# Two layers of attention over an image: key batches taken ahead, the mean taken early, and another order at the end

## The chip, the cores and the metric

The kernel runs on one core of a Trainium2 chip. The metric is the device time of one execution in microseconds (us); the time given for a kernel is the median of its runs. The engines are TensorE (PE, with its weight loads as PEld), VectorE (DVE), ScalarE (ACT), GpSimd (POOL) and SyncE (SP, which issues the DMAs here). Each engine takes its instructions in the order in which the program lists them for it.

## The reference

Two layers run one after the other on x of shape (4, 128, 96, 96), float32. A layer is, with all biases left out here:

```python
g     = maxpool2(conv1x1(x, g_w))        # (b, 64, 2304)
theta = conv1x1(x, theta_w)              # (b, 64, 9216)
phi   = maxpool2(conv1x1(x, phi_w))      # (b, 64, 2304)
attn  = softmax(theta^T phi)             # (b, 9216 queries, 2304 keys)
y     = attn g^T                         # (b, 9216, 64)
x     = batchnorm(conv1x1(y, W_w)) + x
```

So there are eight attention blocks (four images, two layers), each of 9216 queries, 2304 keys and 64 channels.

## The kernel before

The eight blocks run in an order (`ORDER`) that alternates images, so that the keys of a block can be made while the block in front of it runs. A block's queries are cut into nine pairs of 2 x 512 queries (`Pair`), its keys into 18 tiles of 128 (`KT`). A step `t` of the main loop takes one batch of two key tiles (`KB`) for one pair; nine steps (`NB`) make a pair, and 18 steps (`CYCLE`) make a cycle of an even and an odd pair. `s` is the step's place in its cycle. The order of everything is written out by hand in this loop, and each engine keeps it.

In a step, PE computes two tiles of scores (L313) and, for the batch of one step earlier, two tiles of values (L336). All these matmuls have 64x64 tiles, four of which use the four quadrants of the array at once. ACT takes exp of each score tile (L319) from one of two PSUM tiles into one of seven buffers (`EXPS`), with a fixed shift, not with the row's maximum. DVE adds the exps up over the key tiles (L326, L328). Beside that, a cycle holds for the two pairs before it: the two halves of the sum, over the partitions, are brought together by a DMA on SP (`move`, L365) and an addition (`fold`, L369); ones turn them into denominators (L446), ACT copies these out (L360), DVE takes reciprocals in pieces of 128 columns (L356), multiplies (L380), PE projects with W (L386), and DVE adds the shift and x (L395). `note` (L373) sums the reciprocals on ACT for a check at the end: if a sum of exps left the range of float32, a general kernel runs instead.

The keys of a block: PE multiplies a chunk of x by the weights of g and phi into a PSUM tile of a ring of two (`ps_misc`), DVE pools it to 128 keys (L225). From the pooled phi the mean over some keys is taken off, which leaves the softmax as it is: `centring` (L266, L267) takes the mean on DVE, `centred` (L272) subtracts it on ACT, `copied` (L278) puts phi on the other 64 partitions too. `square` (L285) transposes g on DVE in pieces of 32x32 into gT, which the values need. For blocks after the first, `chunks` makes a batch of two key tiles crosswise in 64x64 tiles, half of the contraction in one step, half in the next; the steps are those of `KEYS`. After three batches (`spreads`), phi is centred and copied and g transposed for six tiles at once, and the first time the mean is taken then, over six tiles.

For the first block, two batches of keys are made before the loop by `pooled` (in 128x64 tiles, L238), with theta (L300) between them. In the loop, step t then makes batch t + 2, in the same way, and every third step transposes six tiles of g. In the last cycle, theta of the odd pair (L300) and the denominators of the even pair (L349) have 128x64 tiles; the even pair's reciprocals are taken in a row in step 10 and its projection stands in step 16. After the last scores come the denominators of the last pair, its last two value tiles, and `finish`: copy, add, multiply, project, add x, store in four pieces.

Of the kernel before, what the change touches and what calls it, by code (L numbers as in the profile page):

```python
# [35 lines left out]
NB = NKT // KB  # L36
KEYS = (15, 17, 31)
# [10 lines left out]
def shifted_blocks(ctx: ExitStack, tc: tile.TileContext, x: bass.AP, layers, out: bass.AP, flag):  # L48
# [43 lines left out]
    dens = const.tile([P, len(ORDER) * NP], F32, name="dens")  # L92
    recs = const.tile([P, len(ORDER) * NP], F32, name="recs")
# [109 lines left out]
    class Block:  # L203
# [28 lines left out]
        def pooled(self, j):  # L232

            pss = two_banks(f"gphi_ps_{self.name}_{j}")
            for i in range(2):
                rhs = self.chunk(j * KB + i, slice(0, P))
                for c in range(2):
                    nc.tensor.matmul(  # L238
                        pss[i][ts(c, CI), :], lhsT=self.w.gphi[:, ts(c, CI)], rhs=rhs,
                        start=True, stop=True,  # L240
                    )
            for i in range(2):
                self.pool(j * KB + i, pss[i])
# [35 lines left out]

        def square(self, i, k):  # L280

            tiles = ts(i, GT)
            g = self.gphi[:CI, :].rearrange("p (t k) -> p t k", k=KT)
            for c in range(CI // 32):
                nc.vector.transpose(  # L285
                    self.gT[ts(k, 32), tiles, ts(c, 32)], g[ts(c, 32), tiles, ts(k, 32)]
                )

    class Pair:
# [8 lines left out]
        def theta(self, ps):  # L298
            for h in range(2):
# [3 lines left out]
                )  # L303

# [40 lines left out]
        def denominators(self, ps):  # L345
            parts = [self.sum, self.es[NKT - 1]] if self.last else [self.sum]
            for i, part in enumerate(parts):
                for h in range(2):
                    nc.tensor.matmul(  # L349
                        ps[ts(h, CI), :], lhsT=ones, rhs=part[:, ts(h, QT)],  # L350
                        start=(i == 0), stop=(i == len(parts) - 1),
                    )

# [48 lines left out]
        def finish(self, den, check, result):  # L402

            n = QT // 2
            halves = work.tile([P, PT], F32, tag="halves", name=f"halves_{self.name}")
            y, half = halves[:, :QT], halves[:, QT:]
            nc.scalar.copy(half, self.av[:, QT:])
            nc.vector.tensor_add(y, self.av[:, :QT], half)
            for i in range(2):
                nc.vector.tensor_mul(y[:, ts(i, n)], y[:, ts(i, n)], self.rc[:, ts(i, n)])  # L410
            nc.scalar.activation(
                self.th, den, AF.Identity, accum_out=dens[:, self.number : self.number + 1]
            )
            self.note(self.th)
            pss = [
                ps_sc.tile([P, PT], F32, tag="sc", name=f"W_ps_{self.name}_{i}") for i in range(2)
            ]
            for i in range(2):
                for c in range(2):
                    for h in range(2):  # L420
                        nc.tensor.matmul(
                            pss[i][ts(c, CI), h * QT : h * QT + n],
                            lhsT=self.blk.w.W[ts(h, CI), ts(c, CI)],
                            rhs=y[ts(h, CI), ts(i, n)], start=True, stop=True,
                        )
            check()
            for i in range(2):
                for h in range(2):
# [3 lines left out]
                        dst, pss[i][:, h * QT : h * QT + n], self.blk.w.shift, dst,  # L432
                        op0=ALU.add, op1=ALU.add,
                    )
                    nc.sync.dma_start(out=self.blk.store[:, first : first + n], in_=dst)
                if i == 0:
                    result()

    def denominators(both, folded):
# [3 lines left out]
        def make():  # L443
            for h in range(2):
                for i in range(2):
# [5 lines left out]
        def take():  # L451
            for i in range(2):
                both[i].take_denominators(pss[i], both[i].halves[:, QT:])
# [61 lines left out]
    busy(WARM[1])  # L515
    ws[0].make_theta()
    b0.pooled(0)
    first_cols(ps_sc.tile([P, PT], F32, tag="sc", name="cols_first_ps")[:, :QT])
    th = ps_sc.tile([P, PT], F32, tag="sc", name="theta_ps_0")[:, :QT]
    pairs[0].theta(th)  # L520
    b0.centring(KB)
    b0.centred(ts(0, KB * KT))
    b0.copied(ts(0, KB * KT))
    pairs[0].take_theta(th)
    for w in ws:
        w.make_std()
    nc.scalar.preload_act_table(AF.Exp)
    b0.pooled(1)
    b0.centred(ts(1, KB * KT))
    b0.copied(ts(1, KB * KT))  # L530
# [8 lines left out]
    keys, spreads = {}, {}  # L539
    for n in range(1, len(blocks)):  # L540
        cycle = (n - 1) * NP * NB // CYCLE * CYCLE
        for j in range(NB):
            t = cycle + KEYS[j % len(KEYS)] + j // len(KEYS) * CYCLE
            keys[t] = (n, j)
            if j % len(KEYS) == len(KEYS) - 1:
                spreads[t + 2] = (blocks[n], j // len(KEYS))
    loads = {4 * NB + 4: 2, 31 * NB + 4: 3}
    late = len(pairs) - 2
    folded, gone, pending = None, [], (None, None)
    for t in range(total + 1):  # L550
# [4 lines left out]
        if t in keys:  # L555
            n, i = keys[t]
            if i == 0:
                begin(n)
            first, *pending = blocks[n].chunks(i)
        elif t < total and s == (THETAS if q else THETAS + 2):  # L560
            if q < late:
                first, *pending = thetas(pairs[q + 1 : q + 3])
            else:
                ps = ps_misc.tile([P, QT], F32, tag="misc", name="theta_ps_last")
                first, take = (lambda: odd.theta(ps)), (lambda: odd.take_theta(ps))
        elif gone and s == SUMS:
            second, take = denominators(gone, folded)
        elif gone and s in PROJECT:
            pair = gone[PROJECT.index(s)]
            second, take = pair.multiply, pair.add  # L570
        if t < total:
# [4 lines left out]
            if s == NB and q < late:  # L576
# [13 lines left out]
        if t + 2 < NB:  # L590
            b0.pooled(t + 2)
# [5 lines left out]
        if t + 2 < NB:  # L597
            b0.centred(ts(t + 2, KB * KT))
            b0.copied(ts(t + 2, KB * KT))
            if t % 3 == 0:  # L600
                for k in range(KT // 32):
# [372 lines left out]
```

## Time and profile before

| | |
|---|---|
| median of 3 runs | 2544.60 us (2544.17 to 2545.17) |
| the profiled execution's own time | 2544.58 us |
| its span, first to last instruction | 2542.5 us |
| PE busy | 2525.2 us, 99% |
| DVE busy | 2170.6 us, 85% |
| ACT busy | 1625.2 us, 64% |
| one exp of a score tile (L319) | 1112 ns, 1296 of them |
| one addition of exps (L328) | 1224 ns |
| pooling of a key tile (L225) | 684 ns |
| reciprocal of 128 columns (L356) | 946 ns (3.38 us for four in a row) |

A row of the trace gives start, length, engine, line, operation and tiles; a bracket at its end tells how long the engine was idle before it and which work ended that. A row with xN holds N instructions in a row. A 64x64 matmul of 512 columns appears as two records, so that 16 records are two tiles of scores. Rows of stages give, for each engine, busy time and number of instructions, then the granted clock of PE (1.00 is full speed) and the DMA's share.

### The profile page before, as it was taken

Reading aid. Unit: us, or ns where it says so; the run is one execution under the profiler, and the core shown is the slowest. Engines: PE = TensorE matmul, PEld = TensorE weight load, DVE = VectorE, ACT = ScalarE, POOL = GpSimd, SP = SyncE. Lnnn points to the kernel's source line nnn. Section 1 sums busy time; section 2 is a strip of 40 time slices with the busy share of each in tenths; the row PEclk is TensorE's granted clock in tenths of the full one; section 3 lists DMA queues with packets and bytes.
Section 4 is the critical chain, followed back from the end, with each engine's and each line's share of the span. In section 5 each row is a group of like instructions: output and inputs, shape, how many; then the busy total and the mean of one; then the engine's idle time right before and its main releaser. Section 6 shows DMA issues by size and latency. Waiting matters only on the chain.

```text
span 2542.5 us, 53323 instructions
## 1 busy us (share of the span) xinstructions
PE 2525.2 (99%) x23290; PEld 1380.7 (54%) x23290; DVE 2170.6 (85%) x2258; ACT 1625.2 (64%) x1792; POOL 0.7 (0%) x6
## 2 busy tenths in 40 slices
PE   9999999999999999999999999999999999999998
PEld 3345555455555555555555555555555545555552
DVE  6788888888888888888888888888888888888888
ACT  5666666666666666666666666666666666666665
POOL 0000000000000000000000000000000000000000
PEclk9999999999999999999999999999999999999999
DMA  4020000000000000020000000000000000000000
GB/s 157 6 84 10 10 9 6 9 10 10 10 10 21 26 26 26 14 84 10 10 10 18 13 26 26 26 18 5 10 10 10 18 26 14 26 26 26 26 26 35
DMA packets 16581, 59.86 MB, mean 24 GB/s; under 512 B 2634, under 2 KB 3540, under 8 KB 16340
## 3 DMA queue, kind: packets, MB, share of 16 engines
q1 hardware_dynamic: 16172, 56.31, 7.2%
q8 instruction: 184, 3.01, 0.5%
q14 instruction: 57, 0.47, 0.1%
q10 hardware_dynamic: 168, 0.07, 0.0%
HBM read 19.14 MB, written 18.87 MB: 15 GB/s over the span
## 4 chain that ended last, share of the span: by engine, by line
PE 97%; DVE 2%; ACT 1%; issue 0%; POOL 0%; DVEq 0%; POOLq 0%
PE sc L313 43%; PE av L336 43%; PE gphi_ps L199 4%; PE W_ps L386 2%; PE theta_ps L199 2%; PE den_ps L446 1%; DVE sum L328 1%; ACT exp L319 1%; PE gphi_ps L238 0%; ACT phi L272 0%; DVE centre L266 0%; DVE gT L285 0%; DVE gphi L225 0%; PE warm_ps L508 0%; DVE sum L356 0%
## 5 line engine op out<-in xcount | busy, mean ns | idle before, releaser
L319 ACT ACTIVATE exp<-sc,nshift 128x1024 f32<-128x1024 f32 x1296 | 1384.3, 1112 | 815.3 <-PE sc L313 814.8
L328 DVE TENSOR_TENSOR sum<-sum,exp 128x1024 f32<-128x1024 f32 x1151 | 1408.3, 1224 | 261.9 <-ACT exp L319 208.9
L313 PE MATMUL sc<-theta,phi 64*64 64x512 f32 x10368 | 1470.0, 589 | 0.3 <-ACT theta L307 0.3
L336 PE MATMUL av<-exp,gT 64*64 64x512 f32 x10368 | 1424.7, 589 | 1.0 <-DVE gT L285 1.0
L313 PEld LDWEIGHTS sc<-theta,phi 64*64 64x64 f32 x10368 | 641.3, 133 | 496.4 <-issue 476.2
L336 PEld LDWEIGHTS av<-exp,gT 64*64 64x64 f32 x10368 | 628.9, 133 | 506.9 <-issue 470.2
L356 DVE RECIPROCAL halves<-halves 128x128 f32<-128x128 f32 x280 | 264.9, 946 | 0.0
L199 PE MATMUL gphi_ps<-x,gphiT 64*64 64x512 f32 x1008 | 171.3, 591 | 5.1 <-DVE gphi L225 5.1
L326 DVE TENSOR_TENSOR sum<-exp,exp 128x1024 f32<-128x1024 f32 x72 | 88.1, 1224 | 50.0 <-ACT exp L319 49.6
L225 DVE TENSOR_REDUCE gphi<-gphi_ps 128x128 f32<-128x512 f32 x144 | 93.2, 684 | 39.4 <-PE gphi_ps L199 28.8
L343 ACT COPY halves<-av 128x1024 f32<-128x1024 f32 x71 | 71.9, 1013 | 50.2 <-PE av L336 50.2
L395 DVE SCALAR_TENSOR_TENSOR x<-W_ps,shift,x 128x512 f32<-128x512 f32 x142 | 99.6, 743 | 0.0
L199 PE MATMUL theta_ps<-x,thetaT 64*64 64x512 f32 x560 | 94.4, 589 | 0.0
L199 PEld LDWEIGHTS gphi_ps<-x,gphiT 64*64 64x64 f32 x1008 | 62.2, 132 | 59.1 <-issue 34.1
L386 PE MATMUL W_ps<-halves,WT 64*64 64x512 f32 x568 | 94.2, 589 | 0.0
L369 DVE TENSOR_TENSOR folded<-folded,sum 64x1024 f32<-64x1024 f32 x70 | 85.2, 1216 | 1.1
L285 DVE STREAM_TRANSPOSE gT<-gphi 32x192 f32<-32x192 f32 x192 | 70.7, 368 | 3.6
L386 PEld LDWEIGHTS W_ps<-halves,WT 64*64 64x64 f32 x568 | 36.2, 133 | 27.0 <-issue 27.0
L380 DVE TENSOR_TENSOR halves<-halves 128x512 f32<-128x512 f32 x70 | 48.5, 692 | 2.4
L199 PEld LDWEIGHTS theta_ps<-x,thetaT 64*64 64x64 f32 x560 | 35.6, 133 | 27.2 <-issue 26.9
L446 PE MATMUL den_ps<-folded,ones 64*64 64x512 f32 x280 | 47.1, 589 | 0.0
L377 DVE TENSOR_TENSOR halves<-halves 128x512 f32<-128x512 f32 x71 | 45.7, 684 | 0.0
(89 smaller groups left out, 299.0 us busy)
## 6 DMA issues: line engine op xcount, KB each, us to landing
folded<-sum SPq DMA_DIRECT2D x70, 256.0 KB
out_dram<-x SPq DMA_DIRECT2D x35, 512.0 KB
x<-in_x_dram SPq DMA_DIRECT2D x18, 768.0 KB
x<-in_x_dram SPq DMA_DIRECT2D x12, 384.0 KB
out_dram<-x SPq DMA_DIRECT2D x4, 128.0 KB
gphi_nat<-in_L_conv_phi_w_dram SPq DMA_DIRECT2D x2, 32.0 KB
rows_other<-in_L_conv_g_b_dram SPq DMA_DIRECT2D x4, 0.2 KB
W_nat<-in_L_conv_W_w_dram SPq DMA_DIRECT2D x2, 32.0 KB
```

What stands on the lines that cost most here:

```text
L199: nc.tensor.matmul(out, lhsT=lhsT, rhs=rhs, start=step == 0, stop=step == 1)
L225: nc.vector.tensor_reduce(self.gphi[:, ts(k, KT)].rearrange("p (h w) -> p h w", w=w), ps.rearrange("p (h a w b) -> p h w a b", a=2, b=2, w=w),
L313: nc.tensor.matmul(ps[ts(c, CI), ts(h, QT)], lhsT=self.blk.phi[ts(h, CI), ts(2 * k + c, CI)], rhs=self.th[ts(h, CI), :], start=True, stop= ...
L319: nc.scalar.activation(e, ps, AF.Exp, bias=nshift)
L326: nc.vector.tensor_add(self.sum, self.es[0], e)
L328: nc.vector.tensor_add(self.sum, self.sum, e)
L336: nc.tensor.matmul(self.av[ts(h, CI), ts(r, QT)], lhsT=self.blk.gT[ts(r, CI), k, :], rhs=e[ts(r, CI), ts(h, QT)], start=(k == 0), stop=(k ...
L356: nc.vector.reciprocal(self.rc[:, ts(i, P)], src[:, ts(i, P)])
L369: nc.vector.tensor_add(folded[here, :], folded[here, :], self.sum[here, :])
L386: nc.tensor.matmul(self.pss[h][ts(c, CI), :], lhsT=self.blk.w.W[ts(h, CI), ts(c, CI)], rhs=self.y[ts(h, CI), :], start=True, stop=True,)
L395: nc.vector.scalar_tensor_tensor(dst, self.pss[h], self.blk.w.shift, dst, op0=ALU.add, op1=ALU.add)
L446: nc.tensor.matmul(pss[i][ts(h, CI), :], lhsT=ones[ts(i, CI), :], rhs=folded[ts(i, CI), ts(h, QT)], start=True, stop=True,)
```

## The change

- Before the first scores, six batches of the first block's keys are made (`FIRST = 6`), chunk by chunk with one PSUM tile each; theta of the first pair comes behind them, and the first six tiles of g are transposed there.
- The other three batches are made in the loop, crosswise, by `chunks`, at steps 0, 2 and 4. Their transposes are spread over steps 0 to 6.
- For later blocks, the mean of phi is taken over the first batch alone, two steps behind that batch, and no longer at the first spread.
- In the last cycle, theta of the odd pair and the denominators of the even pair go in 64x64 tiles: the even pair's sum is moved and folded as those of other pairs, and theta's two halves of the contraction lie in two PSUM tiles that DVE adds. The even pair's reciprocals stand in steps 13 to 16, its product in step 16, its projection in step 17.
- In the last three steps, fewer values are computed beside the scores (one tile, one, two); four value tiles remain behind the last denominators, which are made in two halves of 256 columns.
- At the end, both halves of the values are multiplied by the reciprocals straight from PSUM, and the projection adds them up in PSUM. The final check has fewer instructions.

```diff
+FIRST = 6
...
+        def pooled(self, k):
+            ps = ps_misc.tile([P, QT], F32, tag="misc", name=f"gphi_ps_{self.name}_{k}")
+            for c in range(2):
+                nc.tensor.matmul(
+                    ps[ts(c, CI), :], lhsT=self.w.gphi[:, ts(c, CI)],
+                    rhs=self.chunk(k, slice(0, P)), start=True, stop=True,
+                )
+            self.pool(k, ps)
...
+        def batch(self, j):
+            self.centred(ts(j, KB * KT))
+            self.copied(ts(j, KB * KT))
...
+        def theta_alone(self):
+            pss = two_banks(f"theta_ps_{self.name}")
+            def make():
+                for c in range(2):
+                    for r in range(2):
+                        nc.tensor.matmul(
+                            pss[r][ts(c, CI), :], lhsT=self.blk.w.theta[ts(r, CI), :],
+                            rhs=self.blk.xt[ts(r, CI), ts(2 * self.p + c, QT)],
+                            start=True, stop=True,
+                        )
+            def take():
+                self.take_theta(pss[0])
+                nc.vector.tensor_add(self.th, self.th, pss[1])
+            return make, take
...
+        def last_denominators(self):
+            n = QT // 2
+            self.rc, notes = self.sum[:, :QT], []
+            for i in range(2):
+                den = ps_sc.tile([P, PT], F32, tag="sc", name=f"den_last_ps_{i}")[:, :n]
+                for part in (self.sum, self.es[NKT - 1]):
+                    for h in range(2):
+                        nc.tensor.matmul(
+                            den[ts(h, CI), :], lhsT=ones,
+                            rhs=part[:, h * QT + i * n : h * QT + (i + 1) * n],
+                            start=part is self.sum, stop=part is not self.sum,
+                        )
+                notes.append(den)
+            for i in (0, 1):
+                for k in range(n // P):
+                    nc.vector.reciprocal(
+                        self.rc[:, ts(i * n // P + k, P)], notes[i][:, ts(k, P)]
                     )
...
         def finish(self, ...):
-            nc.scalar.copy(half, self.av[:, QT:])
-            nc.vector.tensor_add(y, self.av[:, :QT], half)
             for i in range(2):
-                nc.vector.tensor_mul(y[:, ts(i, n)], y[:, ts(i, n)], self.rc[:, ts(i, n)])
...
+                for r in range(2):
+                    part = slice(r * QT + i * n, r * QT + (i + 1) * n)
+                    nc.vector.tensor_mul(y[:, part], self.av[:, part], self.rc[:, ts(i, n)])
...
+                    for r in range(2):
+                        for h in range(2):
+                            nc.tensor.matmul(
+                                pss[i][h][ts(c, CI), :n],
+                                lhsT=self.blk.w.W[ts(h, CI), ts(c, CI)],
+                                rhs=y[ts(h, CI), r * QT + i * n : r * QT + (i + 1) * n],
+                                start=r == 0, stop=r == 1,
+                            )
...
+    b0.pooled(0)
     ws[0].make_theta()
-    b0.pooled(0)
     first_cols(...)
+    b0.pooled(1)
+    b0.centring(KB)
+    b0.batch(0)
+    for j in range(1, FIRST):
+        for k in range(j * KB, (j + 1) * KB):
+            b0.pooled(k)
+        b0.batch(j)
...
     pairs[0].theta(th)
...
     pairs[0].take_theta(th)
+    for k in range(KT // 32):
+        b0.square(0, k)
...
-    keys, spreads = {}, {}
+    keys = {2 * j: (0, FIRST + j) for j in range(NB - FIRST)}
+    squares = {k: [(1, k)] for k in range(4)} | {k: [(2, 2 * k - 10), (2, 2 * k - 9)] for k in (5, 6)}
+    spreads, centres = {}, {}
...
+            if j == 0:
+                centres[t + 2] = blocks[n]
...
+    ends = {
+        total - 3: (NKT - 8,), total - 2: (NKT - 7,), total - 1: (NKT - 6, NKT - 5),
+        total: range(NKT - 4, NKT),
+    }
...
+        elif q == late and s == 11:
+            second, take = denominators([even], folded)
+        elif t == total - 1:
+            second, take = even.multiply, even.add
...
-            if s == NB and q < late:
+            if s == NB:
                 folded = work.tile([P, PT], F32, tag="folded", name=f"folded_{q}", bufs=1)
                 even.move(folded)
...
+        if q == late and s == 10:
+            even.fold(folded)
...
+        if t - 1 in keys and t < NB:
+            b0.batch(keys[t - 1][1])
...
-            for k in range(j * KB, (j + 1) * KB):
+            for k in ends.get(t, range(j * KB, (j + 1) * KB)):
                 pairs[before].values(k)
...
             if q == late:
                 if s == 10:
-                    den = ps_misc.tile([P, QT], F32, tag="misc", name="den_ps")
-                    even.denominators(den)
-                    even.take_denominators(den, even.sum[:, :QT])
-                    even.inverses(even.rc)
                     even.add_halves()
-                if s == 13:
-                    even.note(even.rc)
+                if s - 13 in range(QT // P):
+                    even.inverses(even.rc, (s - 13,))
+                if s == 16:
                     even.normalise()
-                if s == 16:
-                    even.multiply()
-                    even.add()
...
+        if t in centres:
+            centres[t].centring(KB)
+        for i, k in squares.get(t, []):
+            b0.square(i, k)
...
                 if k == 0:
-                    if i == 0:
-                        blk.centring(GT)
                     blk.centred(ts(i, GT * KT))
```

`second` is issued on PE behind both score tiles of its step and in front of the values; `take` stands on DVE or ACT between the two additions of exps.

## Prediction

> **What bounds the kernel now.** I read the page's busy shares and the shares of its chain, then busy time by stage, then the order of time in the three places where TensorE (PE) is not full: the opening, one spot in each later block, and the end.
>
> ```profile
> PE 2525.2 (99%) x23290; PEld 1380.7 (54%) x23290; DVE 2170.6 (85%) x2258; ACT 1625.2 (64%) x1792; POOL 0.7 (0%) x6
> PE 97%; DVE 2%; ACT 1%; issue 0%; POOL 0%; DVEq 0%; POOLq 0%
> 60.00:342.00 282.00, 281.26 (x2608) 135.40 (x2605) 240.18 (x264) 180.53 (x198) 0.00 (x0) 1.00 0.08 26
> 1752.00:2034.00 282.00, 282.00 (x2633) 165.15 (x2628) 242.29 (x244) 182.98 (x203) 0.00 (x0) 1.00 0.05 11
> ```
>
> PE bounds it; a row of 16 score records (two key tiles) takes 1.72 us, so one unit, four concurrent 64x64 matmuls of 512 columns, is 0.858 us. The change removes no unit in the middle, so it can only win idle or badly filled PE time. The stage rows say that there is little: 0.74 us of idle in the first 282 us window, none in the other shown. The idle sits here:
>
> ```profile
> 160.10 0.95 DVE L266 TENSOR_REDUCE centre<-gphi 64x1 f32<-64x768 f32 x1
> 161.27 0.93 ACT L272 ACTIVATE phi<-gphi,centre 64x768 f32<-64x768 f32 x1 [2.44 <-DVE centre L267]
> 163.48 1.04 PE L313 MATMUL sc<-theta,phi 64*64 64x512 f32 x8
> 164.51 1.28 DVE L225 TENSOR_REDUCE gphi<-gphi_ps 128x128 f32<-128x512 f32 x2
> 165.25 1.25 PE L199 MATMUL gphi_ps<-x,gphiT 64*64 64x512 f32 x5 [0.74 <-DVE gphi L225]
> ...
> 173.46 2.05 PE L313 MATMUL sc<-theta,phi 64*64 64x512 f32 x14
> ...
> 231.65 0.93 ACT L272 ACTIVATE phi<-gphi,centre 64x768 f32<-64x768 f32 x1
> ```
>
> Once per block DVE reduces the mean, ScalarE (ACT) waits 2.44 us for it with the exps behind it, the adds come late, the pooling behind them too, and PE waits for the two PSUM tiles that pooling frees. The last row is the same block's second spread, with the same transposes and pooling but no mean: ACT does not wait, and PE shows no gap after it. The opening and the end:
>
> ```profile
> 7.46 0.69 DVE L225 TENSOR_REDUCE gphi<-gphi_ps 128x128 f32<-128x512 f32 x1 [1.54 <-PE gphi_ps L238]
> 11.45 1.95 PE L313 MATMUL sc<-theta,phi 64*64 64x512 f32 x16 [0.31 <-ACT theta L307]
> 17.33 3.06 DVE L285 STREAM_TRANSPOSE gT<-gphi 32x192 f32<-32x192 f32 x8
> 20.44 1.51 PE L336 MATMUL av<-exp,gT 64*64 64x512 f32 x11 [0.28 <-DVE gT L285]
> 67.89 0.23 PE L110 MATMUL cols_other_ps<-ident,rows_other 11*128 11x11 f32 x1
> ...
> 2503.77 3.38 DVE L356 RECIPROCAL sum<-sum 128x128 f32<-128x128 f32 x4
> 2529.87 3.39 DVE L356 RECIPROCAL sum<-den_last_ps 128x128 f32<-128x128 f32 x4 [2.12 <-PE den_last_ps L349]
> 2534.41 1.09 PE L421 MATMUL W_ps<-halves,WT 64*64 64x256 f32 x16 [2.70 <-DVE halves L410]
> 2536.37 0.85 DVE L431 SCALAR_TENSOR_TENSOR x<-W_ps,shift,x 128x256 f32<-128x256 f32 x2
> ```
>
> **The change part by part.** All sums are against the profiled execution: span 2542.5 us, 2544.58 us with what lies around it, which is the median of the runs (2544.60).
>
> *Opening.* The mark is cols_other (67.89): up to it the same PE work stands in both kernels, and eight units (6.86) and a change of tile shape (0.15) lie between the second pair's first score and the mark, so that score starts at 60.9. From the first keys (5.58) to 60.9 there are 55 units: 18 key chunks, 3 thetas, 18 scores, 16 values, 47.2 us. Before loses 8.1 there.
> After: x lands piece by piece (the first at 5.0, the eighth, which chunk 11 needs, at 14.1, by the trace's landings), in an unchanged order on SP. Chunk 0 starts at 5.2 in front of thetaT, still at the half clock that the records show until about 7 us, and its pooling runs 7.0 to 7.75. Two PSUM tiles rotate, so chunk k+2 waits for the pooling of chunk k: from start to pooled is 1.07 + 0.69, the wait 0.06, hence 0.92 per chunk, slower than PE (0.86) and than x. With the mean (0.42 + 0.15) between poolings 1 and 2, chunk 11 is pooled at 18.9. Then ACT takes the batch (0.50 + 0.40 with issue, 0.94) and only behind it theta (0.69): first score at 20.65, against 11.45. Thirteen units are then done, 42 are left, 36.0 us. Stalls in them: the fourth score waits for an exp, 0.5; the transposes of tiles 12 to 17 stand behind two adds each (2.5) in steps 5 and 6 and end about 52.3, when PE wants them at 51.2, 1.1. The mark's score is at 20.65 + 36.0 + 1.6 = 58.3: **-2.6**. The keys left for the loop run crosswise, in the shape of the scores, so the two changes of shape per step that before pays there are in the 8.1. Bounds: no stall -4.2; the loop at the old pace of 5.47 a step (1.87 keys, 1.88 values, 1.72 scores), no gain.
>
> *Mean early.* It costs DVE 0.57 in a step of 4.29 us that holds 2.5 us of adds and nothing for PE to wait on soon (the next key batch is four steps later); in exchange 1.1 leaves the crowded step. ACT's phi then starts at 158.85 behind its exp, exps run at 160.25, DVE pools at 162.6 and ends at 163.9; PE asks at 164.3. Worth: by idle 0.74 each. By units: from 163.48 to 173.46 lie ten (8.58 us) and 9.98 pass, so 1.4, since one quadrant of PE starts early and three late. The records of the seven blocks agree with the second (from the stall at 165.25 to that at 446.67 are 281.42 us for 326 units, 279.7). I take 1.4: 7 x 1.4 = **-9.8**; bounds -5.2, and 0 if the wait only moves.
>
> *Last cycle.* theta and the even pair's denominators lose their 128x64 shape: two changes each, 2479.12 to 2480.13 for one unit, 0.15 + 0.15, so -0.66 with the other. The sum's halves now go through one more SP transfer (256 KB, 2.8 us to landing elsewhere in the trace; the store in front of it is issued 1.2 us earlier) and a fold of 1.22 on DVE; it lands at 2498.6, DVE arrives at 2498.9: hidden, if late by 1 us, 1 us on DVE. Theta's second half is another 0.69 on DVE, hidden by two steps.
> The cost: reciprocals stand one per step in steps 13 to 16, normalise behind them, and the even pair's projection, which needs it, stands in step 17 right behind the last scores. From the fold on DVE has fold 1.2, 14 adds of 1.27, five reciprocals of 0.83, three short products and sums 1.8, two additions of x 1.3: 26.3, from 2498.9 to 2525.5 with 0.3 of waiting. PE, with two values fewer, ends its last scores at 2522.75. The projection waits: **+2.8**, the values and denominators behind it, and nothing else can run on PE. Bounds +2.4 (DVE never waiting) to +3.3.
> Then the denominators, four value tiles (3.43 us) over the last reciprocals (done 1.2 us before them), and the tail: four products out of PSUM at 0.4 (nearest row 0.38 from SBUF; 0.43 for an addition out of PSUM), projection 1.3 for the first half, four checks 0.65 and additions 0.43: 4.2 us from the last value to the last addition, against 5.5 (2531.71 to 2537.22). -1.3. Copy (0.59) and addition (0.63) of the halves go, as the projection adds them up. The sums for the check, four on ACT of some 0.6 each, end 2533.3, before the last value. The even pair's store comes 2 us later on SP, with 9 us to spare; POOL's queue is as it was. Sum: -0.7 + 2.8 - 1.3 = **+0.9** with rounding.
>
> Total -2.6 - 9.8 + 0.9 = -11.5: span 2531.0, **2533.1 us**.
>
> **A rule that speaks against it.** The 2.70 us gap before the final projection left the clock at full: the 16 records of 256 columns behind it took 1.09 us, as half of 16 score records (0.86) and the last one's end; at half clock it would be over 1.7. The Trainium skill, page "TensorE: Matmul & The Clock Gate", section "Why this matters for your kernels", advises no idle of more than about 3 us between bursts, or the clock falls to half. My new gap is 2.8, with 8 us of PE work behind it. By the row it costs nothing more; by the rule, were the gap counted, one window of about 3.4 us (the same page, "What's actually happening") at half speed, an estimate of +1.7 us, 2534.8. I go by the row, as the gaps are alike; the range keeps the rule.
>
> **The rivals.**
> 1. Only visible idle comes back in the middle (5.2): 2537.7. For it: the stage rows. Against it: the count of units.
> 2. DVE is ready in the last cycle and the projection doesn't wait: 2530.3. For it: DVE shows waits for exps until 2499. Against it: it was behind until 2524.89 in the kernel shown, with its reciprocals in one lump.
> 3. The opening stays at DVE's pace and gains nothing: 2535.7. For it: values waited for gT at 20.44. Against it: 2.5 adds, half of 1.3 pooling, 0.75 transposes, 4 us in a step of 4.29.
> 4. The mean is not what makes pooling late; the stall stays: 2542.9. Against it: the second spread.
> 5. Slower: the 1.8 us without PE work before the first score, at 18.9 to 20.65, comes close behind twelve chunks with small gaps, and the clock falls and stays. At half clock PE loses half of the time, so over 23 us of it turn the sign; 50 us would give 2533.1 + 25 = 2558. Against it: the clock is 1.00 in each stage row, and the longer gap of 2.70 did not lower it.
>
> **How the numbers follow.** Chances: forecast 0.62 (2531 to 2536), rival 1 0.12, rival 2 0.08, rival 3 0.08, rival 4 0.06, rival 5 0.04. 0.2% is 5.1 us, about what a measurement of this kernel tells from no change. Faster than 2539.5 are the forecast and rivals 1 to 3, less 0.04 where 1 and 3 meet: 0.86; the same 0.10, slower 0.04. The range 2530.0 to 2538.5 holds the forecast and the first three rivals but for their tails.
>
> **What would show it.** First score near 20.65 and cols_other near 65.3; no row of PE waiting for pooling in the seven blocks, ACT's phi no longer behind the centre; a PE gap of 2.4 to 3.3 us in front of the last cycle's W_ps; the last addition 4.2 us after the last value. A mark later than 67.9, a wait for gphi in the blocks, or a granted clock under 1.00 would make it wrong.

## The result, and the profile after

Median of the runs: 2533.45 us after (2532.86 to 2535.03), 2544.59 before. The ratio is 0.9957 [0.994, 0.9974]: 11.1 us, or 0.44%, faster. The profiled execution took 2533.95 us, with a span of 2531.9.

The page's busy shares, and the busy time by stage (columns: stretch and length, then PE, PEld, DVE, ACT and POOL busy with their counts, the granted PE clock, DMA share, GB/s):

```profile
PE 2517.3 (99%) x23342; PEld 906.6 (36%) x23342; DVE 2167.9 (86%) x2259; ACT 1627.0 (64%) x1795; POOL 0.7 (0%) x6
```

```profile
58.00:340.00 282.00, 282.00 (x2623) 101.24 (x2621) 241.31 (x266) 180.63 (x197) 0.00 (x0) 1.00 0.08 26
1750.00:2032.00 282.00, 282.00 (x2632) 100.91 (x2628) 242.15 (x245) 182.21 (x200) 0.00 (x0) 1.00 0.05 13
```

PE has no idle time left in the first of these stretches, where before had 0.74. The larger difference is in the column of weight loads (PEld): 135 and 165 us of 282 before, 101 in both stretches now, for practically the same number of loads. The loads themselves are no shorter, as the rows for the scores of the two pages say (before, then after; total busy time, then mean ns of one):

```profile
L313 PEld LDWEIGHTS sc<-theta,phi 64*64 64x64 f32 x10368 | 641.3, 133 | 496.4 <-issue 476.2
L334 PEld LDWEIGHTS sc<-theta,phi 64*64 64x64 f32 x10368 | 398.9, 133 | 714.7 <-issue 650.3
```

One load takes 133 ns in both. The busy time counts loads that run together only once: before, fewer of them ran together, so the four quadrants of the array were out of step.

The order of time after: the opening, then the spot in the second block where PE used to wait.

```profile
5.10 1.08 PE L237 MATMUL gphi_ps<-x,gphiT 128*64 128x512 f32 x4
...
18.68 0.50 ACT L270 ACTIVATE phi<-gphi,centre 64x256 f32<-64x256 f32 x1 [0.94 <-DVE gphi L226]
19.65 0.69 ACT L328 ACTIVATE theta<-theta_ps,cols_first 128x512 f32<-128x512 f32 x1
20.39 1.09 PE L334 MATMUL sc<-theta,phi 64*64 64x512 f32 x8 [1.62 <-ACT theta L328]
...
24.43 1.09 PE L334 MATMUL sc<-theta,phi 64*64 64x512 f32 x8 [0.38 <-ACT exp L340]
...
52.27 1.51 PE L357 MATMUL av<-exp,gT 64*64 64x512 f32 x11 [0.17 <-DVE gT L287]
65.30 0.23 PE L111 MATMUL cols_other_ps<-ident,rows_other 11*128 11x11 f32 x1
...
156.26 0.93 ACT L270 ACTIVATE phi<-gphi,centre 64x768 f32<-64x768 f32 x1
160.04 1.28 DVE L226 TENSOR_REDUCE gphi<-gphi_ps 128x128 f32<-128x512 f32 x2
161.74 1.04 PE L200 MATMUL gphi_ps<-x,gphiT 64*64 64x512 f32 x8
```

The last row answers to the one at 165.25 before: the same keys, with no wait in brackets and as one group of eight instead of five, three and their neighbours mixed in. ACT's phi has no wait either.

The end after, in the order of time:

```profile
2510.41 0.94 DVE L400 RECIPROCAL halves<-halves 128x128 f32<-128x128 f32 x1
2511.39 0.69 DVE L424 TENSOR_TENSOR halves<-halves 128x512 f32<-128x512 f32 x1
2512.13 1.09 PE L430 MATMUL W_ps<-halves,WT 64*64 64x512 f32 x8 [2.68 <-DVE halves L424]
2513.04 3.51 PE L357 MATMUL av<-exp,gT 64*64 64x512 f32 x16
...
2518.39 3.66 PE L357 MATMUL av<-exp,gT 64*64 64x512 f32 x32
2522.61 2.29 PE L460 MATMUL W_ps<-halves,WT 64*64 64x256 f32 x32 [0.55 <-DVE halves L453]
...
2525.16 0.85 DVE L471 SCALAR_TENSOR_TENSOR x<-W_ps,shift,x 128x256 f32<-128x256 f32 x2
```

The predicted wait is there (2.68, with the last reciprocal and normalise right ahead of it on DVE). Something unpredicted stands behind it: 16 values in 3.51 us, where 16 take 1.90 elsewhere. Busy time in three stretches of 3.41 us laid around it tells why:

```profile
2509.77:2513.18 3.41, 1.05 (x12) 0.50 (x16) 3.38 (x4) 1.74 (x4) 0.00 (x0) 1.00 0.02 5
2513.18:2516.59 3.41, 3.41 (x22) 0.67 (x15) 1.44 (x3) 0.00 (x0) 0.00 (x0) 0.50 0.32 130
2516.59:2520.00 3.41, 3.41 (x32) 1.63 (x36) 2.35 (x3) 0.95 (x4) 0.00 (x0) 1.00 0.06 24
```

For 3.41 us behind the gap the granted clock was 0.50. It fell 1.05 us after PE was at work again, and came back after one such stretch.

Where the 10.6 us between the two profiled executions lie, taken between marks that stand in both:

| part | from | us |
|---|---|---|
| up to cols_other (not all of it the opening's own, see below) | 67.89 to 65.30 | -2.6 |
| middle, to values of the last cycle (2481.04 to 2467.22), less the opening and the new shape of theta (0.35) | -13.82 + 2.59 + 0.35 | -10.9 |
| shapes in the last cycle | 0.35 + 0.3 | -0.65 |
| wait for normalise | | +2.7 |
| half clock behind it | projection to last value, 9.93; 8.28 in the repeated run below | +1.65 |
| last value to last addition | 5.51 to 3.96 | -1.55 |
| last addition to the end of the span | 5.28 to 5.89 | +0.6 |

The sum is -10.75, and the spans differ by 10.6.

### The profile page after: what moved, and what is told of

Read it like the earlier page. It is cut to its first block, busy times and chain, and to the rows that moved or that the text cites. A ratio compares the mean times of both kernels' runs of the same rounds, so it can differ in the third digit from the quotient of the medians.

```text
span 2531.9 us, 53451 instructions
## 1 busy us (share of the span) xinstructions
PE 2517.3 (99%) x23342; PEld 906.6 (36%) x23342; DVE 2167.9 (86%) x2259; ACT 1627.0 (64%) x1795; POOL 0.7 (0%) x6
## 4 chain that ended last, share of the span: by engine, by line
## 5 line engine op out<-in xcount | busy, mean ns | idle before, releaser
L334 PE MATMUL sc<-theta,phi 64*64 64x512 f32 x10368 | 1252.3, 589 | 2.0 <-ACT theta L328 1.6
L357 PE MATMUL av<-exp,gT 64*64 64x512 f32 x10368 | 1236.4, 590 | 0.2 <-DVE gT L287 0.2
L357 PEld LDWEIGHTS av<-exp,gT 64*64 64x64 f32 x10368 | 399.8, 133 | 715.4 <-issue 690.7
L334 PEld LDWEIGHTS sc<-theta,phi 64*64 64x64 f32 x10368 | 398.9, 133 | 714.7 <-issue 650.3
L200 PE MATMUL gphi_ps<-x,gphiT 64*64 64x512 f32 x1056 | 137.3, 589 | 0.0
L430 PE MATMUL W_ps<-halves,WT 64*64 64x512 f32 x568 | 74.3, 590 | 2.7 <-DVE halves L424 2.7
L200 PE MATMUL theta_ps<-x,thetaT 64*64 64x512 f32 x560 | 73.6, 589 | 0.0
L200 PEld LDWEIGHTS gphi_ps<-x,gphiT 64*64 64x64 f32 x1056 | 45.1, 132 | 68.3 <-issue 61.2
L417 ACT ACTIVATE halves<-halves 128x512 f32<-128x512 f32 x71 | 44.6, 628 | 1.6 <-DVE halves L424 1.6
L404 ACT ACTIVATE halves<-den_ps 128x512 f32<-128x512 f32 x71 | 41.8, 602 | 1.6 <-DVE halves L421 1.5
```

The lines of the kernel that those rows point to most:

```text
L200: nc.tensor.matmul(out, lhsT=lhsT, rhs=rhs, start=step == 0, stop=step == 1)
L334: nc.tensor.matmul(ps[ts(c, CI), ts(h, QT)], lhsT=self.blk.phi[ts(h, CI), ts(2 * k + c, CI)], rhs=self.th[ts(h, CI), :], start=True, stop= ...
L357: nc.tensor.matmul(self.av[ts(h, CI), ts(r, QT)], lhsT=self.blk.gT[ts(r, CI), k, :], rhs=e[ts(r, CI), ts(h, QT)], start=(k == 0), stop=(k ...
L430: nc.tensor.matmul(self.pss[h][ts(c, CI), :], lhsT=self.blk.w.W[ts(h, CI), ts(c, CI)], rhs=self.y[ts(h, CI), :], start=True, stop=True,)
```

## The experiments

All were run in five rounds, in three groups. The medians of before beside them were 2544.46 (the changed kernel again, the mean taken late, the opening of before, the gap filled), 2544.18 (the values back, the held values in front, the opening trimmed, the last two together) and 2544.63 (the early mean alone, the mean late but short). A comparison with "the unedited kernel" is with the median of its repetition, 2532.69. Every edit is to the changed kernel, except where it says otherwise.

**The changed kernel again**, unedited, for the length of the end.

> The changed kernel once more. In its profile the clock stood at half for 3.41 us, just behind the 2.68 us in which PE waits for the even pair's projection; two of its four runs had a mean clock of 1.000 and took 2532.9 us, two had 0.999 and took 2534.0 and 2535.0. Theory: the half-clock window comes in some executions and not in others, and costs 1.1 to 2.1 us where it does: runs with clock 1.000 stay at 2532.9 (0.2 either way), those with 0.999 lie at 2534 or above. Rival: the spread is unrelated to the clock; then runs with clock 1.000 spread over the whole 2532.9 to 2535 as well.

Measured: 2532.69 us (2531.87 to 2533.59), ratio 0.9954 [0.994, 0.9967]. The order of time on PE:

```profile
2512.07 1.09 PE L430 MATMUL W_ps<-halves,WT 64*64 64x512 f32 x8 [2.68 <-DVE halves L424]
2512.98 1.90 PE L357 MATMUL av<-exp,gT 64*64 64x512 f32 x16
```

The same wait to the last digit, and the values behind it at full speed. Here the stretch that ends just after PE resumes held more work:

```profile
2510.16:2513.57 3.41, 1.50 (x16) 0.67 (x20) 3.32 (x5) 1.29 (x3) 0.00 (x0) 1.00 0.02 5
2513.57:2516.98 3.41, 3.41 (x36) 1.42 (x28) 2.09 (x4) 0.18 (x1) 0.00 (x0) 1.00 0.38 154
```

So the fall of the clock belongs to the execution and not to the kernel: the same gap met the 3.41 us stretches at another place (the section on the prediction takes this up).

The expectation missed: it wanted to tell the two kinds of execution by the mean clock of a run. The quickest run, 2531.87, has a mean of 0.999, and those with 1.000 took 2532.01 to 2532.71. A mean of 0.999 can come from the last 2.6 us alone: in the profiled execution the clock was at half there, behind PE's last work. Only a mean of 1.000 tells something, since it leaves room for at most 2.5 us at half clock (0.0005 of the time, doubled), less than one stretch. By that, six of this kernel's nine runs on record had no half stretch that cost time (five by their mean, one by its trace), one had, and two (2533.59 and 2535.03) can't be told.

**The mean taken late again.**

```diff
-            if j == 0:
-                centres[t + 2] = blocks[n]
...
+                    if i == 0:
+                        blk.centring(GT)
                     blk.centred(ts(i, GT * KT))
```

> The changed kernel with the mean of phi back at the first spread, over six key tiles. Theory: the stall in front of the key chunks comes back in each of seven blocks, and the adds behind it, 1.4 to 1.6 us each: 2543.3 to 2544.3 us, slower by 9.8 to 10.9. Rival (only visible idle counts): 7 x 0.74 = 5.2 slower, 2538.6. Rival (the mean is not the cause): no difference, 2533.4.

Measured: 2544.03 us (2543.46 to 2545.11), ratio 0.9998 [0.9989, 1.0007]. That is 11.3 above the unedited kernel: all of the gain is gone. The view of waits (us in total, times, longest) and the row of PE in the second block are nearly those of before (21.7 and 5.1 us; 0.74):

```profile
ACT phi L270 <- DVE centre L265: 21.4, 8, 4.3
PE gphi_ps L200 <- DVE gphi L226: 5.1, 7, 0.7
```

```profile
162.44 1.25 PE L200 MATMUL gphi_ps<-x,gphiT 64*64 64x512 f32 x5 [0.74 <-DVE gphi L226]
```

Seven waits of PE, 5.1 us in all, cost 11.3. In the traces, from cols_other to the even pair's last projection, 2457.77 us pass here and 2446.83 in the changed kernel: 10.9 more, 1.56 per block.

**The early mean alone**, in the kernel before.

```diff
+            if j == 0:
+                centres[t + 2] = blocks[n]
...
+        if t in centres:
+            centres[t].centring(KB)
...
-                    if i == 0:
-                        blk.centring(GT)
```

> The kernel before, with the early mean alone: over the first batch, two steps behind it. Theory: the seven stalls and what follows them go, 1.55 us each, whatever stands at both ends: 10.9 faster, 2533.4 (0.8 either way). Rival: in the kernel before something else, behind the stall, takes its place: 5 or less faster, 2539 or more.

Measured: 2533.16 us (2532.96 to 2533.53), ratio 0.9955 [0.9941, 0.9969], so 11.5 less than before. The page's busy shares:

```profile
PE 2518.5 (100%) x23290; PEld 899.9 (36%) x23290; DVE 2166.4 (86%) x2258; ACT 1625.4 (64%) x1792; POOL 0.7 (0%) x6
```

One move of two small instructions gives the whole change's time, and the busy time of the loads falls from 1380.7 us to 899.9 with the same 23290 of them. Between cols_other and the last projection the trace is 10.9 shorter than before's (2455.60 for 2466.52). The opening and the last cycle nearly cancel out.

**The mean late, but over two key tiles**, so that DVE spends 0.42 on it instead of 0.95. As in the mean taken late, but with `blk.centring(KB)`.

> The changed kernel with the mean at the first spread again, but over two key tiles (0.42 + 0.15 on DVE, not 0.95 + 0.15). Theory: the place matters, as ACT's phi and the exps behind it wait for DVE's queue: phi starts at 158.0 and not 156.3, the exp behind it 1.2 later, the second pooling ends 162.55 where PE asks at 161.74: 0.8 to 0.9 lost per block, 5.6 to 6.3 in all, 2538.3 to 2539. Rival (DVE's time alone counts): the half of the late mean's cost goes with half of its time, or there is slack for 0.57: 2532.7 to 2535.

Measured: 2540.48 us (2539.33 to 2541.7), ratio 0.9984 [0.9975, 0.9993]: 7.8 above the unedited kernel, and 1.5 above the range that was expected. From cols_other to the even pair's projection 2454.01 us pass, 7.2 more than in the changed kernel: 1.03 per block. The order of time in the second block:

```profile
159.21 0.93 ACT L270 ACTIVATE phi<-gphi,centre 64x768 f32<-64x768 f32 x1 [1.91 <-DVE centre L265]
161.95 1.04 PE L334 MATMUL sc<-theta,phi 64*64 64x512 f32 x8
162.45 1.28 DVE L226 TENSOR_REDUCE gphi<-gphi_ps 128x128 f32<-128x512 f32 x2
163.19 1.25 PE L200 MATMUL gphi_ps<-x,gphiT 64*64 64x512 f32 x5 [0.20 <-DVE gphi L226]
164.10 0.59 PE L334 MATMUL sc<-theta,phi 64*64 64x512 f32 x1
164.27 0.60 PE L200 MATMUL gphi_ps<-x,gphiT 64*64 64x512 f32 x3
164.53 0.77 PE L334 MATMUL sc<-theta,phi 64*64 64x512 f32 x4
```

The wait is 0.20 instead of 0.74, so by idle time this kernel should lose 1.4 us. It loses 7.8. The reason stands in the rows: PE counts as busy once one quadrant works, but three of the four start later, and from there on the four don't run together. One record of the scores, three of the keys, four of the scores: rows of one and three instead of eight and sixteen. The loss can be read off: the unit at 161.95 takes 0.86, so the next was due at 162.81. The row of five begins at 163.19 and lasts 1.25; one of its records takes 0.64, so its last ones began 0.61 after its first, at 163.80. The three late quadrants are 0.99 behind, which is the 1.03 per block. The same sum for the row at 165.25 in before (due at 164.34, last records begun at 165.86) gives 1.52, where the marks give 1.56. The shorter reduction helps by 0.5 per block (1.56 less 1.03); where the mean stands gives the other 1.0.

**The opening of before**, with the rest of the change.

```diff
+    b0.pooled(0)
...
-    for j in range(1, FIRST):
-        for k in range(j * KB, (j + 1) * KB):
-            b0.pooled(k)
-        b0.batch(j)
...
-    keys = {2 * j: (0, FIRST + j) for j in range(NB - FIRST)}
+    keys = {}
...
+        if t + 2 < NB:
+            b0.batch(t + 2)
```

> The changed kernel with the opening of before: two batches of keys in front of the first scores, the rest in the loop in 128x64 tiles. Theory: slower by the 2.6 us by which the mark cols_other moved, 2536.0, and cols_other at 67.9 again. Rival: the opening is worth nothing, as lateness in it is made good later: 2533.4.

Measured: 2537.18 us (2534.7 to 2537.58), ratio 0.9968 [0.9955, 0.998]. The runs lie in two groups, near 2534.8 and 2537.3. The order of time on PE, and the stretches around the wait:

```profile
67.82 0.23 PE L111 MATMUL cols_other_ps<-ident,rows_other 11*128 11x11 f32 x1
2515.76 1.98 PE L430 MATMUL W_ps<-halves,WT 64*64 64x512 f32 x8 [2.97 <-DVE halves L424]
```

```profile
2512.21:2515.62 3.41, 0.58 (x8) 0.00 (x0) 3.27 (x4) 1.90 (x2) 0.00 (x0) 1.00 0.00 0
2515.62:2519.03 3.41, 3.27 (x16) 1.04 (x20) 2.45 (x4) 0.72 (x2) 0.00 (x0) 0.50 0.02 5
```

The median is 4.5 above the unedited kernel's, more than the 2.6 expected. By the marks of these two executions the opening is worth 67.82 - 65.30 = 2.5 us, but in the one the clock reached full later than in the other; like with like, it is 1.5 to 1.8 (see the section on the prediction). The wait for normalise is 0.3 longer. The profiled execution, with the half clock, was the 2537.58 at the top of the slower group, and 3.27 us of PE work at half clock cost 1.6 of the 2.5 between the groups. Of the others, the 2537.20 has a mean clock of 0.998, which asks for at least 7.6 us at half clock, more than the 6.9 between PE's last work and the end in the profile, and the 2534.70 has 1.000, so no half stretch. For the rest the clock is likely but not shown, and the remaining 0.9 between the groups stays open.

**The gap filled**: twelve matmuls in 64x64 tiles whose result nobody reads, issued behind the last scores.

```diff
+        if t == total - 1:
+            odd.fill()
```

> The changed kernel with twelve matmuls of 64x64 tiles and 512 columns (a value tile three times over, into PSUM tiles that nobody reads) between the last scores and the even pair's projection; its result is unchanged. They take 2.57 us and fill the wait of 2.68. Theory (an idle PE lowers its own clock): no half-clock window before the end, every run at 2532.9 (0.2 either way) and the spread of the runs under 0.5 us. Rival (the window is set by something else, as the load before it): half-clock windows come as often as in the changed kernel, and its matmuls are only more: 2533.4 to 2535. The wait itself stays: if it was PE's order and not DVE's lateness that made it, the time grows by 2.6.

Measured: 2532.52 us (2532.18 to 2532.77), ratio 0.9953 [0.9939, 0.9966]. The order of time on PE:

```profile
2510.05 2.85 PE L425 MATMUL fill_ps<-exp,gT 64*64 64x512 f32 x24
2513.09 1.09 PE L442 MATMUL W_ps<-halves,WT 64*64 64x512 f32 x8 [0.20 <-PE fill_ps L425]
2513.97 1.93 PE L357 MATMUL av<-exp,gT 64*64 64x512 f32 x16
```

Three units of added work cost nothing, so the wait is DVE's, and what PE does meanwhile is free. The clock stayed at 1.00 to the end of PE's work, and the runs lie within 0.6 us (under 0.5 was expected) where the unedited kernel's spread over 1.7. With five runs of each, that this spread comes from the clock is likely, not shown.

**The values back in their old steps.**

```diff
-    ends = {
-        total - 3: (NKT - 8,), total - 2: (NKT - 7,), total - 1: (NKT - 6, NKT - 5),
-        total: range(NKT - 4, NKT),
-    }
+    ends = {}
```

> The changed kernel with the values in the last three steps as in all others (two tiles per step, two left behind the last denominators). Theory: what makes PE wait for the even pair's projection is DVE, which reaches the product at its own time; the two value tiles taken out of steps 15 and 16 only make the hole wider. With them back the wait shrinks from 2.68 to about 0.95, never lowers the clock, and the last value ends 2 us earlier; but the last reciprocals are then 1 us late for the products: the last addition comes 1.3 us earlier than in an execution of the changed kernel at full clock, 2530.5 to 2531.5 us. Rival (the delayed values are what hides the last reciprocals and are worth it, as their place suggests): slower by 1 to 2, 2533.5 to 2534.5.

Measured: 2531.3 us (2530.64 to 2531.63), ratio 0.9949 [0.9936, 0.9963]. The order of time on PE:

```profile
2512.15 1.09 PE L430 MATMUL W_ps<-halves,WT 64*64 64x512 f32 x8 [1.13 <-DVE halves L424]
...
2519.74 2.29 PE L460 MATMUL W_ps<-halves,WT 64*64 64x256 f32 x32 [1.03 <-DVE halves L453]
```

The wait for normalise shrinks by 1.55, since PE comes later to it. The wait before the final projection grows by 0.5, since fewer values cover the last reciprocals. The two make 1.1, and the medians lie 1.4 apart: holding the values back, as the change does it, costs and does not gain.

**The held values in front of the projection**: 12 to 14 behind the last scores, then the projection, three values behind the denominators.

```diff
-        total - 3: (NKT - 8,), total - 2: (NKT - 7,), total - 1: (NKT - 6, NKT - 5),
-        total: range(NKT - 4, NKT),
+        total - 3: (NKT - 8,), total - 2: (NKT - 7,), total - 1: (NKT - 6, NKT - 5, NKT - 4),
+        total: range(NKT - 3, NKT),
...
-        elif t == total - 1:
-            second, take = even.multiply, even.add
...
         if t == total - 1:
+            even.multiply()
+            even.add()
             odd.last_denominators()
```

> The changed kernel with three value tiles (12 to 14) between the last scores and the even pair's projection, and three left behind the last denominators. Nothing else moves. Theory: the projection starts when DVE has its product, as now (2512.07 in the profile with full clock), but PE works until 0.1 us before; the denominators start at 2513.2, the last value ends at 2517.8, the last addition 2.5 us earlier than now: 2529.7 (0.6 either way), no half-clock window. Rival (DVE's own chain, adds, product, additions of x, reciprocals, sets the end, not PE's wait): under 1 us faster, 2531.7 or more.

Measured: 2530.1 us (2529.21 to 2530.64), ratio 0.9945 [0.9932, 0.9959]. PE no longer waits for the even pair, and the last gap is as short as in the changed kernel:

```profile
2508.91 2.85 PE L357 MATMUL av<-exp,gT 64*64 64x512 f32 x24
2511.86 1.09 PE L430 MATMUL W_ps<-halves,WT 64*64 64x512 f32 x8
...
2518.23 2.29 PE L460 MATMUL W_ps<-halves,WT 64*64 64x256 f32 x32 [0.55 <-DVE halves L453]
```

The held values do their work if something that waits for DVE stands behind them. As changed, they stood behind the wait.

**The opening trimmed**: theta is taken before the sixth batch on ACT, and the transposes of the last tiles come in one step.

```diff
+        if j == FIRST - 1:
+            th = ps_sc.tile([P, PT], F32, tag="sc", name="theta_ps_0")[:, :QT]
+            pairs[0].theta(th)
+            pairs[0].take_theta(th)
         b0.batch(j)
...
-    squares = {k: [(1, k)] for k in range(4)} | {k: [(2, 2 * k - 10), (2, 2 * k - 9)] for k in (5, 6)}
+    squares = {k: [(1, k)] for k in range(4)} | {5: [(2, k) for k in range(4)]}
```

> The changed kernel with two moves in its opening: ACT takes theta of the first pair in front of the sixth batch's phi and not behind it, and all eight transposes of the last six key tiles stand in step 5 and not in steps 5 and 6. Theory: the first score comes 0.9 us earlier (19.4), and the wait of the values for gT at 52.2 (1.1) goes: 2.0 us earlier at cols_other (63.3), 2530.4 to 2530.8 us. Rival (the opening is bound by DVE's sum of work): the mark moves by under 0.5.

Measured: 2531.12 us (2530.72 to 2532.0), ratio 0.9949 [0.9935, 0.9963]. The order of time on PE:

```profile
19.82 1.09 PE L334 MATMUL sc<-theta,phi 64*64 64x512 f32 x8 [0.79 <-ACT theta L328]
50.52 1.97 PE L357 MATMUL av<-exp,gT 64*64 64x512 f32 x16
63.58 0.23 PE L111 MATMUL cols_other_ps<-ident,rows_other 11*128 11x11 f32 x1
```

The mark comes 1.7 earlier (2.0 was expected), 0.6 of it at the first score and 1.2 between that and the values that had waited for gT, though that wait shows only 0.17 of idle. The time is 0.3 above the expected range. In the profiled execution, the slowest of the five, the clock was at half from 2511.15 to 2514.56, as in the changed kernel's first profile.

**The last two together.**

> Both of the last two: the values ahead of the projection, and the two moves in the opening. The theory has them in different places of PE's chain, so they add: 2.0 + 2.5 below an execution of the changed kernel at full clock (2532.2): 2527.7 (0.8 either way). If one makes up for the other: 2529.5 or more.

Measured: 2527.87 us (2527.32 to 2528.66), ratio 0.9937 [0.9923, 0.995]. The end of PE's order of time:

```profile
2516.64 2.29 PE L460 MATMUL W_ps<-halves,WT 64*64 64x256 f32 x32 [0.55 <-DVE halves L453]
```

This beats both kernels: 16.3 us below before in its own rounds, and 4.8 below the unedited changed kernel of the first rounds. Its clock reached full at 4.40, as in the changed kernel's profile (4.39), and cols_other stands at 63.44: between these two the trimmed opening gives 1.9. It keeps the change's three parts and moves only which instruction stands ahead of which.

## Why the prediction was right, and where its terms were off

The total held (2533.1 predicted, 2533.45 measured) with its range. That rests in part on errors that cancel.

- *Opening, -2.6:* the number came out, in part by luck. The first score came at 20.39 (20.65 predicted) and the mark at 65.30 (65.3), with the forecast waits for an exp and for gT. But the prediction reckoned with the half clock of the start until about 7 us, as in before. In the profiled execution after it, full speed came at 4.39, so the first keys took 1.08 us (row at 5.10). In other executions with the same opening it came later, as in the kernel with the gap filled (6.98; a warm-up matmul takes 0.42 us ahead of such a time and 0.27 behind it):

```profile
5.29 1.90 PE L237 MATMUL gphi_ps<-x,gphiT 128*64 128x512 f32 x4
7.99 2.95 PE L237 MATMUL gphi_ps<-x,gphiT 128*64 128x512 f32 x12 [0.45 <-DVE gphi L226]
66.17 0.23 PE L111 MATMUL cols_other_ps<-ident,rows_other 11*128 11x11 f32 x1
```

The table has the time at which each trace's record of the granted clock first says full:

| kernel | opening | full clock from | first score | cols_other |
|---|---|---|---|---|
| before | old | 7.13 | 11.45 | 67.89 |
| opening of before | old | 6.83 | 11.37 | 67.82 |
| early mean alone | old | 5.21 | 10.59 | 67.04 |
| changed | new | 4.39 | 20.39 | 65.30 |
| changed, again | new | 4.78 | 20.33 | 65.24 |
| gap filled | new | 6.98 | 21.25 | 66.17 |
| mean late, short | new | 7.45 | 21.46 | 66.37 |

Where full speed came late in both, the new opening gains 1.5 to 1.7 us; where it came early, 1.8. The term was too large by some 0.9, and the early clock of the one execution made that good. One missed step shows in the second of the three rows: the transpose of theta's weights takes the second tile of the ring, so chunk 1 already waits for the pooling of chunk 0 (0.45), where the prediction let only chunk k+2 wait for chunk k. Rival 3 falls all the same.
- *Mean early, -9.8:* the right mechanism, a little undersized. The marks give -10.9, taking it back costs 11.3, and doing it alone brings 11.5, or 1.56 per block by the marks (up to 1.64 by the medians) instead of 1.4. The term was found by counting units up to the row at 173.46, which begins with the quadrant that is ahead: its record before that stands alone at 173.03, and the three others' at 173.20, 0.17 behind it. 1.4 and 0.17 make the 1.57 by which these three are late. Out of step as they are, the units keep their pace (281.42 us from one stall to the next is the 279.7 of 326 units and one such loss), so the loss is that of the restart alone. Rival 1, the visible idle, gave 5.2; the kernel with a short late mean refutes it most clearly, losing 7.8 us with 0.20 us of idle per block. Rival 4 falls with the early mean alone.
- *Wait for normalise, +2.8:* 2.68, within its bounds of 2.4 and 3.3. Rival 2 falls: DVE is late even with its reciprocals spread over four steps.
- *The gap costs nothing more:* this step failed in the profiled execution, where it cost 1.7, and held in the one that was profiled again. The row it went by (2.70 before the final projection, clock at full) was the wrong kind of evidence. The granted clock changes at whole multiples of 3.4133 us from its first record: in the profiled execution the fall at 2513.18 is 735 of them (2508.80 us) behind the rise at 4.39, the half clock lasted one, the next fall came four later. In before such a boundary fell at 2533.00, inside the gap, and cut it into 1.3 and 1.4. The clock did fall at the next boundary, 2536.41, with 2.20 us of that stretch idle, but PE's last work was over. Of the stretch that ends at 2513.18 after, 2.36 us were idle, and the clock fell. In the repeated run at most 1.91 us of the gap lay in one stretch, and it did not; in the kernel with the old opening it was 2.83, and it fell. All twelve traces fit: from full speed, the clock fell at the end of each stretch with 2.20 us or more without PE work (so too at 2.66 with the mean late and 2.67 with the trimmed opening, both profiled with half clock), and at the end of none with 1.95 or less. So it was not the gap's length against a limit but its share of one stretch, and two equal gaps are not alike. The Trainium skill, page "TensorE: Matmul & The Clock Gate", section "What's actually happening", describes such a free-running window; its section "Why this matters for your kernels" puts the limit at gaps of about 3 us. These runs agree with the first and ask for a tighter limit than the second: 2.68 was enough. The prediction's own price for it (+1.7) was right (1.65), and it belonged in the sum as a chance, not at nothing.
- *Tail, -1.3:* -1.55 (3.96 from the last value to the last addition, 4.2 predicted). Shapes -0.66: -0.65. Unpriced: 0.6 more from the last addition to the end of the span.
- *Rival 5:* the clock did not fall in the opening, although PE waited 1.62 us there. Its mechanism came once at the end, for 3.41 us, and recovered by itself.

Hence, in the profiled execution: the middle brought 1.1 more than predicted, the tail 0.25 and the wait 0.1 more; the half clock took 1.65 and the end of the span 0.6. That makes 0.8 of the 0.85 by which it lay above the forecast. Without the half clock, and with the 1.65 that the opening gains at a late clock (67.82 less 66.17) in place of 2.6, the same parts add up to -11.45 (an estimate from the figures above), against -11.5: the oversized opening and the undersized middle cancel.

What stays open is whether the two runs without a trace and with a mean clock of 0.999 had the half clock, and what, beside the wait of 0.45, made the first score 0.6 to 0.8 later than 20.65 where full speed came at 7.0 to 7.5 us.

## What to carry to other kernels

Where PE works in four quadrants, price a wait by counting units of work against the clock on both sides of it, for the quadrants that start last, not by the idle time that the profile shows, and look at the busy time of the weight loads: more of it at an unchanged count and length of the loads was here the trace of quadrants out of step. Work that is held back to cover a wait must be issued in front of the instruction that waits; behind it, it is only late. A small instruction on a secondary engine is best moved to a step whose next reader is far away: two DVE instructions per block were worth as much here as the whole of a change in many parts.

## What the runs showed of the hardware that was not expected

- A 2.68 us gap of PE lowered the granted clock to 0.50 for 3.41 us in one execution and not in another of the same kernel. In the twelve traces the clock fell behind stretches of 3.41 us with 2.20 us or more without PE work, and not behind those with 1.95 or less; what holds between is not shown. The fall came at the end of a 3.41 us stretch, in that execution 1.05 us after work had resumed; in the kernel with the old opening it came 0.14 us before. Twelve unused matmuls (2.57 us of work) in a gap that had to be waited out kept the clock up at no cost.
- A wait that shows 0.20 us of idle cost 1.0 us, and one that shows 0.74 cost 1.6, because three quadrants restart 0.6 us after the first. Over the whole kernel the busy time of the weight loads was 1381 us in that condition and 900 us without it, with the same 23290 loads (those of the scores took 133 ns each in both).
- With the same warm-up code, full speed came between 4.39 and 7.45 us after the start. The first keys then took 1.08 or 1.90 us, and a mark at 65 to 68 us moved with it by 0.9 to 1.1 (67.04 to 67.89 with the old opening, 65.24 to 66.37 with the new).
